# Loads of a streaming kernel in runs of four rows instead of eight

## The chip, the core and the metric

The kernel runs on one core of one Trainium2 chip. The metric is the device time of one execution in microseconds (us); the number that counts is the median of several executions. Engines are called PE (TensorE, the matrix unit), DVE (VectorE), ACT (ScalarE), POOL (GpSimd) and SP (SyncE). Sixteen DMA engines move data between the chip's memory and the core's on-chip memory of 128 partitions.

## The reference

```python
x = -7.109e-05 + 0.9999 * jax.random.normal(..., (128, 128, 1024), jnp.float32)
itok_B_0_7 = jax.random.randint(..., (128,), 0, 8, jnp.int32)
weights = jax.random.normal(kw, (8, 128, 128), dtype=jnp.float32) * (1.0 / 128 ** 0.5)

def reference(x, itok_B_0_7, weights):
    w = weights[itok_B_0_7]
    return x + jnp.einsum('bct,bcd->bdt', x, w)
```

For each of 128 images b, a matrix of 128 channels by 1024 samples, one of eight 128 x 128 weight matrices is picked by an index; the image is multiplied by it and added to the product. Input and output are 64 MiB each, all in 32-bit floats.

## The kernel before

**Tiles and slots.** The 128 images are worked through in 32 tiles of four. A tile is 2 MiB (2.097 MB): two halves (`H = 2`) of two images (`G = 2`). The on-chip buffer `x_all` has 12 slots (`SLOTS`) of one tile each, 16 KB in every partition. A tile is loaded into a slot, multiplied from there into PSUM, copied back from PSUM over its own input in the slot, and stored from there. Tile i + 12 takes the slot of tile i when that is stored.

**Loading** (`load`, L147). Each half is one transfer of 1 MiB, issued by ACT in L72 (`transfer`); it is queue q10 in the profile. In the chip's memory the two images of a half are one unbroken stretch of 256 rows of 4 KB (a row is one channel's 1024 samples). The transfer names the stretch as runs of `ROWS` rows, and the target as 128 partitions with 8 KB each. Eight rows are 32 runs of 32 KB, each written to four partitions in a row. Whatever the run, partition p below 64 gets channels 2p and 2p + 1 of the half's first image, and partition 64 + p those of the second.

**Trading** (`trade`, L162). The multiplication needs the channels of one image spread over all 128 partitions. So ACT exchanges, with five copies in L157 by way of a spare buffer, the second row of the lower 64 partitions for the first row of the upper 64. An image then has its even channels below and its odd ones above; the rows of the weights have been brought into the same order at the start.

**ACT's loop** (L275 to L293). At the start ACT issues the loads of four tiles (`AHEAD = 4`). Then for each tile n it waits until both halves have landed, waits until the slot for tile n + 4 is empty (POOL counts the stores that have landed and raises `s_empty`, L311 to L313), issues the two loads of tile n + 4, and trades tile n. What stands there:

```python
landed(k)
with nc.scalar.If(turn < NT // AHEAD - 1):
    empty = nc.scalar.wait_ge(s_empty, k + 1)
...
    load(k, (turn * AHEAD + (k + AHEAD)) % SLOTS, ...)
trade(k, (turn * AHEAD + k) % SLOTS)
```

**Computing.** DVE adds the picked weight matrix to a unit matrix (`place`, L195 to L200), so that the sum with x comes out of the same product. PE multiplies, 16 matmuls a tile (`multiply`, L202, L208), and DVE copies the product to the slot (`copy`, L217, L223).

**Storing** (`store`, L174). SP waits for DVE and issues the stores; they are in queue q1, as are the weights and indices at the start. Tile 0 goes with a plain transfer (L319), whose pieces are the 4 KB rows of the output. Tiles 1 to 19 go one at a time, 2 MiB in runs of 16 KB (on-chip side), the last twelve in pairs, 4 MiB; the last six tiles (`WHOLE = 6`) are named as runs of 32 KB. In the chip's memory every store writes rows of 4 KB. The end of the program waits for the stores.

Of the kernel before, what the change touches and what calls it, by code (L numbers as in the profile page):

```python
# [45 lines left out]

IDLE = 8

ROWS = 8

R = 2

# [33 lines left out]
def kernel(  # L86
# [60 lines left out]
    def load(k, slot, first):  # L147
        for h in range(H):
# [3 lines left out]
                x_all[:, bass.ds(slot * (H * G * T) + h * G * T, G * T)],  # L152
                x[bass.ds(first + h * G, G)].rearrange("h (b r) t -> (h b) (r t)", r=ROWS),
            ).then_inc(s_in[k], DMA)
# [225 lines left out]
```

## Time and profile before

| what | before |
|---|---|
| median of three executions | 323.84 us (323.23 to 324.43) |
| the profiled execution's own time | 323.75 us |
| its span in the trace | 321.9 us |
| PE busy, share of the span | 247.3 us, 77% |
| ACT busy | 195.7 us, 61% |
| DVE busy | 181.4 us, 56% |
| read and written in the chip's memory | 67.63 MB and 67.11 MB, 419 GB/s over the span |

The profile is of one execution; its own time is 1.85 us more than its span, for what lies around the traced instructions. In the page's second part the span is cut into 40 slices of 8 us, and a digit is the busy share in tenths. In the third part each DMA queue has a row: packets, MB, and the time of its packets as a share of 16 engines' span. A packet is one piece of a transfer on one of the 16 DMA engines; those of a few bytes, 16 to a transfer, carry no data. The same rows can be had for any stretch of the span (a window); a packet is counted in the window in which it begins. "ACTq" and "SPq" are DMA issues of ACT and SP.

### The profile page before, as it was taken

Reading aid. Unit: us, or ns where it says so; the run is one execution under the profiler, and the core shown is the slowest. Engines: PE = TensorE matmul, PEld = TensorE weight load, DVE = VectorE, ACT = ScalarE, POOL = GpSimd, SP = SyncE. Lnnn points to the kernel's source line nnn. Section 1 sums busy time; section 2 is a strip of 40 time slices with the busy share of each in tenths; the row PEclk is TensorE's granted clock in tenths of the full one; section 3 lists DMA queues with packets and bytes.
Section 4 is the critical chain, followed back from the end, with each engine's and each line's share of the span. In section 5 each row is a group of like instructions: output and inputs, shape, how many; then the busy total and the mean of one; then the engine's idle time right before and its main releaser. Section 6 shows DMA issues by size and latency. Waiting matters only on the chain. (4 is left out here: it accounts for less than half of the span.)

```text
span 321.9 us, 2680 instructions
## 1 busy us (share of the span) xinstructions
PE 247.3 (77%) x528; PEld 102.7 (32%) x528; DVE 181.4 (56%) x217; ACT 195.7 (61%) x162; POOL 2.5 (1%) x10
## 2 busy tenths in 40 slices
PE   7279988888888888759949799496784989999000
PEld 3034333333333333324314343242332434443000
DVE  4708765666666666663634847266552676787300
ACT  1577767776777776677275772747727689990000
POOL 0200000000000000000000000000000000000000
PEclk9969999999999999998978979799996999999755
DMA  8999999999999999999999999999999999999995
GB/s 326 391 456 444 405 390 430 438 430 432 417 421 432 425 428 428 432 452 407 425 423 425 423 423 419 421 428 438 446 423 405 432 450 403 428 446 432 419 432 220
DMA packets 7732, 134.76 MB, mean 419 GB/s; under 512 B 1457, under 2 KB 1458, under 8 KB 2098
## 3 DMA queue, kind: packets, MB, share of 16 engines
q1 hardware_dynamic: 4658, 67.64, 49.8%
q10 hardware_dynamic: 3072, 67.11, 49.0%
q14 instruction: 2, 0.02, 0.0%
HBM read 67.63 MB, written 67.11 MB: 419 GB/s over the span
## 5 line engine op out<-in xcount | busy, mean ns | idle before, releaser
L208 PE MATMUL ps<-x_all,w 128*128 x512 | 238.8, 624 | 49.0 <-PEq L204 48.8
L223 DVE COPY x_all<-ps 128x2048 f32 x64 | 146.7, 2292 | 113.7 <-PE ps L208 107.4
L208 PEld LDWEIGHTS ps<-x_all,w 128*128 128x128 f32 x512 | 99.1, 199 | 188.6 <-issue 188.3
L157 ACT COPY aside<-x_all 64x1024 f32 x64 | 66.7, 1042 | 82.4 <-issue 79.1
L157 ACT COPY x_all<-aside 64x1024 f32 x64 | 66.8, 1044 | 1.8
L157 ACT COPY x_all<-x_all x32 | 60.7, 1897 | 3.9
L197 DVE TENSOR_TENSOR w<-w_all,eye 128x128 f32<-128x128 f32 x132 | 31.8, 283 | 0.8 <-issue 0.8
L235 PE MATMUL ps<-x_all 128*128 128x512 f32 x16 | 8.6, 697 | 1.7 <-DVE x_all L232 1.7
L235 PEld LDWEIGHTS ps<-x_all 128*128 128x128 f32 x16 | 3.6, 230 | 5.8 <-issue 4.2
L273 ACT ACT_TABLE_LOAD x1 | 1.3, 1283 | 6.2 <-issue 6.2
L299 DVE COPY w_all<-x_all 32x256 f32<-32x256 f32 x12 | 3.9, 326 | 0.4
L244 DVE STREAM_TRANSPOSE x_all<-x_all 128x512 f32<-128x512 f32 x2 | 2.0, 1076 | 3.1 <-DMA x_all<-in_L_cond_weights_dram 3.1
L299 POOL COPY w_all<-x_all 32x256 f32<-32x256 f32 x4 | 1.7, 425 | 6.6 <-DVE x_all L296 6.4
L296 DVE STREAM_TRANSPOSE x_all<-x_all 128x1024 f32<-128x1024 f32 x1 | 1.2, 1226 | 0.0
L232 DVE MEMSET x_all<- 128x512 f32 x1 | 0.5, 485 | 1.0 <-SPq L225 1.0
L250 DVE TENSOR_SCALAR x_all<-x_all 1x128 int32<-1x128 int32 x1 | 0.2, 215 | 0.3 <-DMA x_all<-in_itok_B_dram 0.3
L260 POOL TENSOR_SCALAR_AFFINE_SELECT eye<-x_all 128x128 f32<-128x128 f32 x1 | 0.3, 292 | 1.4 <-DVE x_all L232 1.4
L254 DVE CUSTOM_DVE_ANT_0 index<-x_all 1x256 uint16<-1x256 uint16 x1 | 0.3, 278 | 0.0
L260 POOL TENSOR_SCALAR_AFFINE_SELECT eye<-eye 128x128 f32<-128x128 f32 x1 | 0.3, 292 | 0.1
L252 DVE TENSOR_SCALAR x_all<-x_all 1x128 int32<-1x128 int32 x1 | 0.2, 215 | 0.0
L273 ACT COPY mark<-eye 1x1 f32<-1x1 f32 x1 | 0.2, 190 | 0.0
L367 POOL MEMSET const-bfloat16-1.0<- 128x1 bf16 x1 | 0.1, 101 | 0.0
(5 smaller groups left out, 0.4 us busy)
## 6 DMA issues: line engine op xcount, KB each, us to landing
x_all<-in_x_dram ACTq DMA_DIRECT2D x64, 1024.0 KB, 11.7
out_dram<-x_all SPq DMA_DIRECT2D x20, 2048.0 KB, 54.1
out_dram<-x_all SPq DMA_DIRECT2D x6, 4096.0 KB, 31.4
x_all<-in_L_cond_weights_dram SPq DMA_DIRECT2D x1, 512.0 KB, 3.8
x_all<-in_itok_B_dram SPq DMA_DIRECT2D x1, 0.5 KB
```

What stands on the lines that cost most here:

```text
L157: nc.scalar.copy(out, in_).then_inc(s_moved, 1)
L197: copy = nc.vector.tensor_tensor(ws[q], w_all[:, bass.ds(subject[q], 1), :], eye, ALU.add)
L208: mm = nc.tensor.matmul(ps[h][:, q % G, t : t + N], ws[q][:, 0, :], x_all[:, bass.ds(at, N)], start=True, stop=True,)
L223: nc.vector.tensor_copy(mine, ps[h].rearrange("d g t -> d (g t)")).then_inc(s_added, 1)
L232: nc.vector.memset(zeros, 0.0).then_inc(s_zeros, 1)
L235: nc.tensor.matmul(ps[P_SLOTS - 1][:, G - 1, :N], zeros[:, :D], zeros, start=True, stop=True)
L244: nc.vector.transpose(w_mid.rearrange("p (e r h w j) -> p r j h e w", e=4, r=R, h=4, w=8)[:, r], w_raw.rearrange("p (j r d) -> p r j d", r ...
L254: nc.vector.tensor_tensor(index[:, :B], near, wrap, ALU.add).then_inc(s_index, 1)
L260: nc.gpsimd.affine_select(eye[:, 0], eye[:, 0] if r else zeros[:, :D], [[-1, D]], ALU.not_equal, 1.0, base=r - r * R * A, channel_multipli ...
L273: nc.scalar.copy(mark, eye[:1, 0, :1])
L296: nc.vector.transpose(w_late, w_mid).then_inc(s_sort, 1)
L299: engine.tensor_copy(w_all[32 * v : 32 * (v + 1), 2 * o : 2 * (o + 1), :], w_late[32 * o : 32 * (o + 1)].rearrange("c (e u r d) -> c u r e ...
```

## The change

```diff
@@ -46,7 +46,7 @@
 
 IDLE = 8
 
-ROWS = 8
+ROWS = 4
 
 R = 2
```

`ROWS` is used in one place, in `load`:

```python
x[bass.ds(first + h * G, G)].rearrange("h (b r) t -> (h b) (r t)", r=ROWS)
```

The source of each of the 64 loads is now 64 runs of 16 KB instead of 32 runs of 32 KB. The target is as before, 128 partitions of 8 KB, so a run is written to two partitions instead of four. Which bytes lie in which partition does not change, and neither does any instruction's place on any engine: number, order and waits are the same.

## The prediction

> **What bounds the kernel now.** I read the page's second part first, for the one resource that has no gap, then its third part for what that resource carries.
>
> ```profile
> DMA  8999999999999999999999999999999999999995
> DMA packets 7732, 134.76 MB, mean 419 GB/s; under 512 B 1457, under 2 KB 1458, under 8 KB 2098
> q1 hardware_dynamic: 4658, 67.64, 49.8%
> q10 hardware_dynamic: 3072, 67.11, 49.0%
> x_all<-in_x_dram ACTq DMA_DIRECT2D x64, 1024.0 KB, 11.7
> out_dram<-x_all SPq DMA_DIRECT2D x20, 2048.0 KB, 54.1
> ```
>
> The 16 DMA engines are busy from the second slice to the last but one. q10 is the loads: 67.11 MB, which is 64 transfers of 1,024 KB. q1 is the stores and, at the start, the weights. Together their packets take 98.8% of 16 engines' span, so all idleness is 1.2% of 321.9 us, 3.9 us. A load lands 11.7 us after its issue, a store 54.1 us after: stores queue up, loads do not. The windows (DMA share last but one, GB/s last) say where the idleness lies.
>
> ```profile
> core 0: us, PE busy (x) PEld busy (x) DVE busy (x) ACT busy (x) POOL busy (x), PEclk, DMA share, GB/s
> 10.00:30.00 20.00, 12.26 (x25) 5.09 (x24) 9.24 (x20) 14.47 (x13) 0.79 (x2) 0.83 1.04 446
> 60.00:120.00 60.00, 52.09 (x119) 21.70 (x118) 38.75 (x45) 43.82 (x37) 0.00 (x0) 1.00 1.00 429
> 120.00:260.00 140.00, 111.70 (x231) 46.21 (x230) 76.56 (x85) 87.30 (x72) 0.00 (x0) 0.91 1.00 425
> 298.00:318.00 20.00, 0.00 (x0) 0.00 (x0) 2.69 (x3) 0.00 (x0) 0.00 (x0) 0.59 0.99 424
> 318.00:321.90 3.90, 0.00 (x0) 0.00 (x0) 0.00 (x0) 0.00 (x0) 0.00 (x0) 0.50 0.06 25
> ```
>
> A share over 1 comes of packets that began in the window and ended behind it. From 10 to 318 us the DMA engines have nothing to spare; TensorE has (52.09 of 60 us), and from 298 us on it does nothing at all while stores drain. So the time is the engines' work divided by 16, plus a start and an end of a few us. A change that adds engine work shows in full; a change that only moves loads and stores against each other shows nothing, as long as one of the two queues always has work.
>
> **The price of one packet.** In these windows one kind of packet runs alone: loads (10 to 30 us), single stores (268 to 288), the last stores, whose runs in the chip's memory are 32 KB long (290 to 318).
>
> ```profile
> DMA packets 400, 8.91 MB, mean 446 GB/s; under 512 B 128, under 2 KB 128, under 8 KB 128
> q10 hardware_dynamic: 400, 8.91, 103.7%
> ...
> DMA packets 555, 8.57 MB, mean 428 GB/s; under 512 B 32, under 2 KB 32, under 8 KB 32
> q1 hardware_dynamic: 555, 8.57, 100.9%
> ...
> DMA packets 398, 11.88 MB, mean 424 GB/s; under 512 B 35, under 2 KB 35, under 8 KB 35
> q1 hardware_dynamic: 398, 11.88, 99.5%
> ```
>
> Without the tiny packets under 512 B, the loads are 400 - 128 = 272 packets for 8.91 MB, 32,768 bytes each: a packet is one run of eight rows, so halving the run should double the packets. One takes 20 x 16 x 1.037 / 272 = 1.220 us on its engine. The single stores are 523 packets of 16,384 bytes, 20 x 16 x 1.009 / 523 = 0.617 us. The last stores are 363 packets of 32,768 bytes, 28 x 16 x 0.995 / 363 = 1.228 us.
>
> **What the change removes and adds.** 64 loads x 32 = 2,048 packets of 32 KB go, 128 on each engine; 4,096 of 16 KB come. No row shows a 16 KB load, so I bound it. Above: the 16 KB store, 0.617 us; two make 1.234, 14 ns over the 1.220 us that they replace, and 128 x 14 ns = 1.8 us. Below: two halves cost what the whole did, 0 us. Less than nothing would need a 16 KB packet under 0.610 us, and no row has one. Between the two, by how many pieces a packet is written in: the 32 KB store goes to eight pieces of 4 KB and takes 8 ns longer than the 32 KB load, which goes to four of 8 KB; that is an estimated 2 ns a piece. The new load writes two pieces where the 16 KB store writes four, so 0.617 - 0.004 = 0.613 us, 2 x 0.613 - 1.220 = 6 ns for each old packet, and 128 x 6 ns = 0.8 us. I take 0.9 us, a little towards the row that is nearest, and keep 0 to 1.8.
>
> The Trainium skill, page "DMA: Bandwidth & Descriptors", section "Why small descriptors are slow (HBM only)", speaks against the change too, but by less: it states a fixed overhead of about 3 cycles for each packet on trn2. At the 850 MHz that the same page's section "Where 436 GB/s comes from" gives for the fabric, 128 more packets on an engine would cost an estimated 0.45 us and the forecast would be 0.45 us lower. That overhead alone gives 3.5 ns where the stores' rows leave room for 14, so the rows decide.
>
> **Do the two queues hinder each other when mixed?** This matters because loads and stores will alternate more finely.
>
> ```profile
> DMA packets 1406, 25.72 MB, mean 429 GB/s; under 512 B 304, under 2 KB 304, under 8 KB 304
> q10 hardware_dynamic: 692, 15.34, 59.6%
> q1 hardware_dynamic: 714, 10.39, 40.8%
> ```
>
> In 60 to 120 us, 15.34 MB are 468 loads of 32 KB, 60 x 16 x 0.596 / 468 = 1.223 us each, and 10.39 MB are 634 stores, 0.618 us each: the prices of the runs alone. I cost the alternation at nothing.
>
> **What moves: the shares.** When both queues have work, how is it divided? From 31 to 36 us the loads still have a backlog and the first store, the only one cut into 4 KB packets, has just begun.
>
> ```profile
> DMA packets 119, 1.88 MB, mean 375 GB/s; under 512 B 19, under 2 KB 19, under 8 KB 67
> q10 hardware_dynamic: 70, 1.67, 80.2%
> q1 hardware_dynamic: 48, 0.20, 9.8%
> ```
>
> 1.67 MB is 51 loads of 32 KB, beside 48 stores of 4 KB: a packet each in turn, whatever its size. So a load of 32 KB now has two thirds of the engines against 16 KB stores; with 16 KB it will have half. ScalarE issues a tile's two loads when an earlier tile lands and a slot is free:
>
> ```profile
> 43.01 1.27 ACTq L72 DMA_DIRECT2D x_all<-in_x_dram  x2
> ...
> 51.24 1.31 ACTq L72 DMA_DIRECT2D x_all<-in_x_dram  x2
> ...
> 59.51 1.16 ACTq L72 DMA_DIRECT2D x_all<-in_x_dram  x2
> ...
> 67.70 1.15 ACTq L72 DMA_DIRECT2D x_all<-in_x_dram  x2
> ```
>
> A tile every 8.2 us. Its four packets per engine take 4 x (1.220 + 0.617) = 7.3 us in turns with stores, so the load queue empties before the next tile. After the change eight turns take 8 x (0.613 + 0.617) = 9.8 us: loads will queue, ScalarE will in the end wait for landings, and stores will get through sooner. If issuing a load with twice the runs costs ScalarE more, that is covered: even doubled (1.15 us more per tile) its turn of 8.2 us stays under 9.8. Only the very first issue has nothing before it; I allow 0.6 us for that at the top of the range.
>
> None of this costs time unless both queues run dry before the end. The danger is the end, so I work out how far loads will be ahead of stores.
>
> ```profile
> q10 hardware_dynamic: 538, 11.96, 90.1%
> ...
> q1 hardware_dynamic: 142, 0.58, 14.5%
> ...
> x_all<-in_x_dram ACTq DMA_DIRECT2D x20, 1024.0 KB, 12.2
> ...
> q1 hardware_dynamic: 1059, 22.07, 93.7%
> q10 hardware_dynamic: 14, 0.00, 0.0%
> ...
> 283.77 2.11 ACT L157 COPY aside<-x_all 64x1024 f32 x2 [0.51 <-ACTq L160]
> ...
> 301.24 0.56 SPq L72 DMA_DIRECT2D out_dram<-x_all  x1
> ```
>
> The first row is 0 to 31 us: 11.96 MB are loaded when the first store begins. The second is 31 to 41 us: 142 packets of the first store, 4 KB each, take 10 x 16 x 0.145 / 142 = 0.163 us. The third is 0 to 56 us: 20 loads, ten tiles, are issued. The next two are 266.7 us to the end: now all loads are in by 266.7 us and 22.07 MB, 10.5 tiles of 2.097 MB, are still to be stored. The last two are the last tile's trade and the last store's issue, 17.5 us apart.
>
> After the change the first store's 512 packets of 4 KB are 32 turns on each engine. They take 32 x (0.613 + 0.163) = 24.8 us, in which 512 loads of 16 KB bring 8.39 MB. At 56 us 20.3 MB are loaded (the ten tiles issued are 20.97 MB, so the queue does not run dry) and 2.1 MB stored: 18.2 MB, 8.7 tiles, ahead. From there both sides move 16 KB a turn and the lead stays 8.7 tiles; with 12 slots some 3.3 tiles of loads remain queued, so the load queue stays full. Stores alone take 8 packets of 32 KB per engine and pair of tiles, 8 x 1.228 = 9.8 us, 4.9 us a tile, so the last load lands 8.7 x 4.9 = 43 us before the end, at some 279 us, and the last store can be issued at about 279 + 17.5 + 0.6 = 297 us. It needs 9.8 us, to 307; the stores ahead of it keep the engines busy until about 322 - 9.8 = 312. Nothing shows.
>
> **The sum.** The profiled execution took 323.75 us, 1.85 more than its span. Plus 0.9 it is 324.65 us. The median of the three runs is 323.84, 0.09 above it; for the measured time I give 324.7 us.
>
> **The rivals.** (1) The engines run dry at the end. Last trade to end of last store is 17.5 + 0.6 + 9.8 = 28 us, 5.7 tiles of stores. If the lead after the change falls below 5.7 tiles, each missing tile costs 4.9 us. Loads build most of their lead against the small packets of the first store; if they gained nothing there, the lead would stay at what was loaded by 31 us, 11.96 / 2.097 = 5.7 tiles, just at that point, and whenever the load queue was then empty for a moment it would shrink. One tile less is 4.9 us lost, 329.6 us. For it: the share of the loads does fall, and ScalarE's wait for landings is new. Against it: 3 tiles of margin, and the 51 to 48 packets. Chance 0.1. The Trainium skill, same page, section "Queues, rings and completion order", would rule it out: an engine drains a whole packet, typically 9 to 17 descriptors, from one queue before it turns, so a load's share would hang less on the length of its run. The row of 51 to 48 shows turns of one run each; I go by it.
> (2) The change does not reach the engines, because a transfer of 1 MB is cut as before: 323.8 us. Against it, 32,768 bytes is exactly the run in the code. Chance 0.07.
> (3) Packets of 16 KB are cheaper as loads than any row shows, or finer alternation helps: at 0.600 us a packet, 128 x 20 ns = 2.6 us less, 321.2 us. Against it, mixed and unmixed packets cost the same now. Chance 0.05.
>
> **How the numbers follow.** The forecast, 324.7 us, has 0.78, with a range of its own from 323.8 to 325.6, or 326.2 with the first issue. A difference of 0.5%, 1.6 us, is about what a measurement of this kernel can tell from no change; the three runs lie 1.2 us apart. So slower takes rival (1) and the upper end of the forecast, 0.1 + 0.13 = 0.23; faster is rival (3), 0.05; the rest is 0.72. The range, 323.2 to 326.8 us, holds the forecast, its bounds with the runs' spread, and rival (2), and leaves out most of rivals (1) and (3).
>
> **What would show it.** Right: 4,096 packets of 16 KB in q10 with a price of 0.610 to 0.617 us; the two queues' shares together up by some 0.9 us of span; loads landing far later than 11.7 us and stores sooner than 54.1; the last load near 279 us instead of 266.7; a DMA row without a new gap. Wrong: a 0 or a low digit in the DMA row ahead of the last slice (rival 1), q10 with 32 KB packets as before (rival 2), or a 16 KB load under 0.610 us (rival 3).

## The result and the profile after

The changed kernel takes 335.75 us (median of six runs, 334.82 to 336.24), the kernel before 323.31 us on the same chip (six runs, 322.84 to 324.43). The ratio is 1.0378, with a 95% interval of 1.0365 to 1.0391: 12.4 us slower. The profiled execution took 336.02 us, its span is 334.2 us.

The page of the changed kernel comes first, with the same rows that the prediction showed of the kernel before.

```profile
DMA  7999999999999999999999999999999999997047
DMA packets 9780, 134.76 MB, mean 403 GB/s; under 512 B 1457, under 2 KB 1458, under 8 KB 2098
q1 hardware_dynamic: 4658, 67.64, 47.8%
q10 hardware_dynamic: 5120, 67.11, 47.2%
x_all<-in_x_dram ACTq DMA_DIRECT2D x64, 1024.0 KB, 25.7
out_dram<-x_all SPq DMA_DIRECT2D x20, 2048.0 KB, 35.6
```

q10 has 2,048 packets more, so the runs did reach the engines as packets of 16 KB. Both queues together take 95.0% of 334.2 us, 317.5 us, against 98.8% of 321.9, 318.0 us, before: within the rounding of these shares (0.05% of the span each) the engines have no more work than they had. What is new is the 0 near the end of the DMA row, where the kernel before had nines. The windows show it in microseconds.

```profile
core 0: us, PE busy (x) PEld busy (x) DVE busy (x) ACT busy (x) POOL busy (x), PEclk, DMA share, GB/s
10.00:300.00 290.00, 233.33 (x491) 96.08 (x490) 164.78 (x193) 188.18 (x155) 0.34 (x1) 0.94 1.01 428
300.00:308.00 8.00, 3.67 (x9) 1.33 (x7) 5.38 (x6) 4.93 (x4) 0.00 (x0) 0.90 0.93 395
308.00:322.00 14.00, 8.92 (x16) 3.63 (x16) 5.38 (x6) 1.14 (x2) 0.00 (x0) 0.82 0.01 2
322.00:334.20 12.20, 0.00 (x0) 0.00 (x0) 0.00 (x0) 0.00 (x0) 0.00 (x0) 0.56 0.80 344
```

Up to 300 us the engines run as before. From 308 to 322 us they move nothing: 14 us, a little more than the kernel lost. In that stretch PE does its 16 matmuls of the last tile. These are the last instructions of ACT and SP around it; the three points stand for rows left out:

```profile
302.90 2.11 ACT L157 COPY aside<-x_all 64x1024 f32 x2 [9.66 <-ACTq L160]
...
321.70 0.56 SPq L72 DMA_DIRECT2D out_dram<-x_all  x1
```

ACT waits 9.66 us for the last tile to land (L160 is `landed`) and trades it at 302.90; the last store goes out at 321.70. All other stores were done well before it went out. This is what the first rival of the prediction described: the engines run dry at the end. What remains is why the last load landed at some 301 us, and not at 279 as forecast. The window of 70 to 270 us of the changed kernel, in which both queues have work, answers it.

```profile
DMA packets 6174, 85.69 MB, mean 428 GB/s; under 512 B 944, under 2 KB 944, under 8 KB 944
q1 hardware_dynamic: 3087, 45.34, 53.4%
q10 hardware_dynamic: 3087, 40.36, 47.3%
```

The number of packets is the same in both queues, to the last one, but only if the packets of a few bytes are counted. (Of the data alone it is 40.36 MB / 16,384 = 2,463 packets against 2,767.) So a queue gets one packet in its turn, and the few bytes with which each transfer ends on each engine are a packet like any other; they are called ending packets below. A tile's data is 2,097,152 / 16 = 131,072 bytes on an engine. With four-row loads that is eight packets, and two transfers end: ten turns, 13.1 KB a turn (a KB here is 1,000 bytes). A tile stored alone is eight packets and one end: nine turns, 14.6 KB. The rows have 40.36 MB / 3,087 = 13.1 KB and 45.34 / 3,087 = 14.7 KB. With eight-row loads a tile has 4 + 2 = 6 turns, by the same count 21.8 KB a turn. Before, loads outran stores (15.34 MB against 10.39 in 60 to 120 us); now stores outrun loads by some 12%, and the lead of the loads melts.

The lead, loaded less stored tiles, can be followed in three windows of the changed kernel: 0 to 56 us, 280 to 300.8 us, and 300.8 us to the end.

```profile
q10 hardware_dynamic: 1455, 19.12, 80.9%
q1 hardware_dynamic: 735, 3.62, 16.8%
...
q1 hardware_dynamic: 240, 6.26, 70.6%
q10 hardware_dynamic: 225, 2.90, 32.7%
...
q1 hardware_dynamic: 242, 6.88, 48.4%
q10 hardware_dynamic: 1, 0.00, 0.0%
```

At 56 us it is 19.12 - (3.62 - 0.52 of weights) = 16.0 MB, 7.6 tiles, where 8.7 were forecast. From 70 to 270 us stores gain 45.34 - 40.36 = 4.98 MB, 2.4 tiles. From about 280 us on the last six tiles are being stored in runs of 32 KB, twice the size of a load's, and in 21 us stores gain another 6.26 - 2.90 = 3.36 MB, 1.6 tiles. Another 0.4 tiles go in the two short stretches between (56 to 70 and 270 to 280 us). When the last load has landed, 6.88 MB are left, 3.3 tiles. The prediction put the point of decision at 5.7 tiles and 4.9 us on each that is missing: (5.7 - 3.3) x 4.9 = 11.8 us. The loss is 12.4 us.

### The profile page after: what moved, and what is told of

Same layout as the page of the kernel before. It is cut to its first block, busy times and chain, and to the rows that moved or that the text cites. A ratio compares the mean times of both kernels' runs of the same rounds, so it can differ in the third digit from the quotient of the medians.

```text
span 334.2 us, 2680 instructions
## 1 busy us (share of the span) xinstructions
PE 254.2 (76%) x528; PEld 104.7 (31%) x528; DVE 181.2 (54%) x217; ACT 195.7 (59%) x162; POOL 2.5 (1%) x10
## 5 line engine op out<-in xcount | busy, mean ns | idle before, releaser
L208 PE MATMUL ps<-x_all,w 128*128 x512 | 245.0, 635 | 62.6 <-PEq L204 62.6
L208 PEld LDWEIGHTS ps<-x_all,w 128*128 128x128 f32 x512 | 100.9, 202 | 206.6 <-issue 206.5
L235 PE MATMUL ps<-x_all 128*128 128x512 f32 x16 | 9.3, 742 | 1.7 <-DVE x_all L232 1.7
## 6 DMA issues: line engine op xcount, KB each, us to landing
x_all<-in_x_dram ACTq DMA_DIRECT2D x64, 1024.0 KB, 25.7
out_dram<-x_all SPq DMA_DIRECT2D x20, 2048.0 KB, 35.6
```

The source lines that it names most:

```text
L208: mm = nc.tensor.matmul(ps[h][:, q % G, t : t + N], ws[q][:, 0, :], x_all[:, bass.ds(at, N)], start=True, stop=True,)
L235: nc.tensor.matmul(ps[P_SLOTS - 1][:, G - 1, :N], zeros[:, :D], zeros, start=True, stop=True)
```

## The experiments

Theory T: engines serve the two queues a packet in turn, the ending packets counted; four-row loads therefore lose the lead that eight-row loads build, the last tile lands late, and the engines stand dry while it is traded, multiplied and copied. Rival P: loads in short runs are slow by themselves. Rival S: shares are even, and only the 32 KB stores at the end take the loads' turns.

Each ratio below is to the kernel before as measured together with that run: 323.53 us for the first four runs, 323.81 us for the last four. What a run loses or gains is taken from there.

**The last stores in shorter runs.** On the changed kernel:

```diff
-WHOLE = 6
+WHOLE = 0
```

> Four-row loads as in the changed kernel, and the last six tiles are stored in runs of 16 KB instead of 32 KB. Theory T (each queue gets one packet in turn, the few-byte completion packets included; the loads of the changed kernel therefore fall behind the stores, the last tile lands late, and the engines run dry while it is computed): from 280 us on, loads keep their 203 KB per ns-ten-thousandth share, that is 2.03 MB in 10 us instead of 1.4, so the 2.90 MB that land after 280 us need 14 us instead of 20; the last load at about 294 us, the time about 330 us (329 to 332). Rival P (loads in 16 KB runs are slow by themselves, whatever the stores do): no change, 335.8 us. Rival S (only the 32 KB stores at the end take the loads' share; before that queues share evenly): nearly all of the loss goes, 325 us.

(The garbled "203 KB per ns-ten-thousandth share" stands for 203 GB/s, which is 2.03 MB in 10 us.) Measured: 330.65 us (327.98 to 331.74), ratio to the kernel before 1.0201 (1.014 to 1.0261). The window 280 to 296.5 us of this run:

```profile
q1 hardware_dynamic: 268, 4.13, 58.8%
q10 hardware_dynamic: 227, 2.93, 41.7%
```

The 2.93 MB are in after some 16 us instead of 20.8 (T had expected 14), and the loss falls from 12.4 to 7.1 us, by 5.3. The time lies in T's range of 329 to 332 us. P, which expected no gain, does not fit, and neither does S, by which nearly all would have come back.

**Stores in runs of 8 KB.** On the changed kernel, in `store`:

```diff
-                "d (o t) -> d o t", o=1 if i >= NT - WHOLE else n
+                "d (o t) -> d o t", o=n * 2
```

> Four-row loads, and every store from tile 1 on is cut into runs of 8 KB, half of before. Theory T: a tile of loads is 8 + 2 turns, of stores 16 + 1, so loads get 13.1 KB a turn against 7.7 and never fall behind; no dry stretch; 323.3 plus 0.8 us for the loads' packets and some 2 us for the stores' additional packets: 326 us (325 to 328). Rival P: not under 335.8, and about 338 with the stores' shorter runs. Rival S: 326 us as well.

Measured: 323.22 us (323.07 to 323.73), ratio 0.9990 (0.9978 to 1.0002). The whole loss is gone, although the loads are those of the changed kernel and only the stores were cut. Its page:

```profile
DMA  7999999999999999999999999999999999999995
q1 hardware_dynamic: 9010, 67.64, 50.2%
q10 hardware_dynamic: 5120, 67.11, 49.1%
x_all<-in_x_dram ACTq DMA_DIRECT2D x64, 1024.0 KB, 11.4
out_dram<-x_all SPq DMA_DIRECT2D x20, 2048.0 KB, 54.1
```

Loads land after 11.4 us and stores after 54.1, much as they did before the change. So P falls; S expected the same as T here. The 2 to 3 us that were expected for the additional packets did not come, and the time lies below T's range of 325 to 328 us.

**Four more turns behind each store.** Run lengths stay as in the changed kernel. SP issues a transfer of 48 pieces of 4 bytes from `weights` to an unused buffer (declared with its semaphore in lines not shown); nothing of the computation changes.

```diff
                 store(i, n).then_inc(s_slot[i % SLOTS], DMA)
+                transfer(
+                    nc, nc.sync, tiny[:, i : i + 1], weights[0, :48, :1]
+                ).then_inc(s_tiny, DMA)
```

> Four-row loads and stores as in the changed kernel; behind each store from tile 1 on SP issues one transfer of 192 bytes, which puts three packets of 4 bytes and a completion packet on each engine's store queue. No run length changes. Theory T: a single store has 13 turns instead of 9, a pair 21 instead of 17, so loads (10 turns a tile) get 13.1 KB a turn against 10.1 (12.5 in pairs) and no longer fall behind; no dry stretch, or one of a few us; 325 us (324 to 328). Rivals P and S: packets of a few bytes do not count, 335.8 us or a little more.

Measured: 323.27 us (323.11 to 323.41), ratio 0.9989 (0.9978 to 1.0000). Its window of 70 to 270 us, and then 269 us to the end:

```profile
q10 hardware_dynamic: 3423, 44.81, 52.5%
q1 hardware_dynamic: 3999, 40.70, 48.2%
...
q1 hardware_dynamic: 1270, 20.89, 92.9%
```

Now loads move more than stores, though no run has another length than in the changed kernel, and by 269 us all loads are in, with 20.89 MB, ten tiles, left to store. (The counts are not equal here; the loads of this run land 11.9 us after their issue, as before the change, so the load queue is at times empty.) Packets that carry next to nothing take away the whole loss of 12.4 us, which of the three only T allows. The time, 323.27 us, is below T's range of 324 to 328 us.

**Eight-row loads with four more turns.** This is the reverse, on the kernel before: ACT issues the same small transfer behind the two loads of each tile.

```diff
             ).then_inc(s_in[k], DMA)
+        transfer(
+            nc, nc.scalar, tiny[:, bass.ds(at, 1)], weights[0, :48, :1]
+        ).then_inc(s_tiny, DMA)
```

> Eight-row loads and stores as in the kernel before; behind the two loads of each tile ACT issues one transfer of 192 bytes, three packets of 4 bytes and a completion packet on each engine's load queue. Theory T: a tile of loads has 4 + 2 + 4 = 10 turns, as many as with four-row loads, and so the same 13.1 KB a turn against the stores' 14.6; the loads fall behind, the last load lands near 300 us, and the time is that of the changed kernel less its 0.8 us of packets: 335 us (332 to 337). Rivals P and S: runs of 32 KB are what they were, 323.3 to 324.5 us.

Measured: 336.38 us (334.09 to 336.91), ratio 1.0378 (1.0327 to 1.043), the same ratio as that of the change. Its page's DMA row, the window of 70 to 270 us, and 303 us to the end:

```profile
DMA  8999999999999999999999999999999999979147
...
q1 hardware_dynamic: 3062, 45.19, 53.2%
q10 hardware_dynamic: 3075, 40.31, 47.5%
...
q1 hardware_dynamic: 259, 7.44, 55.2%
```

The loads are those of before, 32 KB a packet; the turns are those of the change, and so are the bytes (45.19 to 40.31 MB, in 3,062 to 3,075 packets) and the time, with a 1 in the DMA row where the engines stand dry at the end. The length of the runs matters here only through the number of turns.

**Runs of two rows.**

```diff
-ROWS = 4
+ROWS = 2
```

> Loads in runs of two rows, 8 KB, half again; stores as in the changed kernel. Theory T: a tile of loads is 16 + 2 turns and the loads' share falls further, but stores can only go out for tiles that have been loaded and computed, so the loss has a floor that the changed kernel has nearly reached: when the last load lands, the last two pairs at the most are left to store. 67.1 + 0.5 + 58.7 MB have then passed at 0.4285 MB per us, with 2.5 us for the additional packets some 300 us, and the rest takes the 35 us that it takes in the changed kernel: 335 us (333 to 338). Rival P (short runs are slow by themselves): at least another 12 us, twice that for twice the packets: 348 to 360 us.

Measured: 336.93 us (335.62 to 338.21), ratio 1.0418 (1.0372 to 1.0463): a loss of 13.1 us, which its interval does not tell from the 12.4 of four rows. Its page:

```profile
DMA  7999999999999999999999999999999999999047
q10 hardware_dynamic: 9216, 67.11, 47.8%
x_all<-in_x_dram ACTq DMA_DIRECT2D x64, 1024.0 KB, 31.4
out_dram<-x_all SPq DMA_DIRECT2D x20, 2048.0 KB, 12.9
```

A store now lands 12.9 us after its issue: there is hardly a backlog of stores left to lose, and the gap cannot grow much. The time lies in T's range; P, by which each halving costs another 12 us or more, is out.

**The last pair split.** On the changed kernel, tiles 30 and 31 are stored one by one, each when DVE is done with it (the wait for the stores at the end is changed to match):

```diff
+            if i + n == NT:
+                nc.sync.wait_ge(s_added, (NT - 1) * H)
+                store(i, 1).then_inc(s_slot[i % SLOTS], DMA)
             nc.sync.wait_ge(s_added, (i + n) * H)
...
-    last = store(NT - PAIR, PAIR)
+    last = store(NT - 1, 1)
```

> Four-row loads; the last pair of tiles is stored as two tiles, each when it is ready, so that only 2.1 MB wait for the last tile instead of 4.2. Theory T: at the end the engines are dry until the last tile is computed, so tile 30 is stored in the dry time, and the last store takes 4.9 us instead of 9.8: 335.75 less 4.9 is 330.9 us (329.5 to 332). Rival P: the engines' work is what it was, 335.8 us.

Measured: 331.26 us (330.19 to 332.12), ratio 1.0227 (1.0195 to 1.026): a loss of 7.5 us, 5.0 less than the changed kernel's. With the 16 KB runs at the end as well:

> Four-row loads, the last pair split as in the run before, and the last six tiles stored in runs of 16 KB instead of 32. Theory T: the two repairs act on different terms, the landing of the last load and the chain behind it, so they add up: 330.65 (16 KB runs alone) less 4.9 is 325.8 us (324 to 327.5). Rival P: 330 us or more.

Measured: 325.10 us (322.90 to 326.06), ratio 1.0028 (0.9999 to 1.0057). The two repairs gained 5.3 and 5.0 us one by one and 11.2 together; the runs of this one spread over 3 us, so the sum fits. The control is the split on the kernel before:

> The kernel before, eight-row loads, with the last pair split. A control for the split. Theory T: with eight-row loads the engines never run dry, so a shorter last store brings nothing: 323.4 us (322.9 to 324). If the split helps here too, its gain with four-row loads is not that of the dry time.

Measured: 323.67 us (322.95 to 324.11), ratio 0.9996 (0.9986 to 1.0007). A shorter chain behind the last load gains where the engines are dry, and nothing where they are not. The DMA rows are from the pages of the split alone, of the split with 16 KB runs, and of the control:

```profile
DMA  7999999999999999999999999999999999999905
...
DMA  7999999999999999999999999999999999999976
...
DMA  8999999999999999999999999999999999999995
```

No version beats the kernel before: the stores of 8 KB and the additional turns behind the stores come back to it, and its engines have hardly any time left to win.

## Why the prediction was wrong

**What bounds the kernel: right.** The engines' packets fill the span but for a start and an end, and a gap at the end shows in full. Loads now queue and stores get through sooner, as forecast: they land after 25.7 and 35.6 us, where it was 11.7 and 54.1.

**The price of the packets: too high.** 0.9 us were forecast, 317.5 against 318.0 us of engine work were measured, and the run with four more turns, which has the same loads, is not slower than the kernel before. Over the whole span a 32 KB load took 321.9 x 16 x 0.490 / 2,048 = 1.232 us before, and a 16 KB load takes 334.2 x 16 x 0.472 / 4,096 = 0.616 us now: two of them 1.232, which adds nothing: the lower bound, 0 us, that the prediction gave for this term. The new price lies in the forecast's 0.610 to 0.617 us. The old one, 1.220 us, was too low: it came from one short window, and the windows differ by about as much as the 6 to 14 ns that the estimate turned on. The prediction's own mixed window, 60 to 120 us, had 1.223 us. From before, 120 to 260 us:

```profile
q10 hardware_dynamic: 1376, 29.89, 50.2%
```

29.89 MB are 912 loads, 140 x 16 x 0.502 / 912 = 1.233 us each. (The 32 KB runs of the last stores, which the prediction puts in the chip's memory, are on the on-chip side; in the chip's memory every store writes rows of 4 KB. Its estimate of 2 ns a piece goes by those rows.) The Trainium skill, page "DMA: Bandwidth & Descriptors", section "Why small descriptors are slow (HBM only)", would have asked for an estimated 0.45 us more. No run here shows even that.

**The shares: the step that failed.** "From there both sides move 16 KB a turn and the lead stays 8.7 tiles". It rested on 51 load packets beside 48 of the store, counted without the packets of a few bytes, in a window that had begun before the first store reached the engines. From before, 33.2 to 42 us, when both queues had work:

```profile
DMA packets 290, 3.75 MB, mean 426 GB/s; under 512 B 48, under 2 KB 48, under 8 KB 192
q10 hardware_dynamic: 144, 3.15, 84.3%
q1 hardware_dynamic: 144, 0.59, 16.6%
```

144 to 144, the 48 small ones of the loads included. That row was there to be read before the change was tried, and ten turns against nine follow from it. The lead did not stay 8.7 tiles: it was 3.3 when the last load was in, at 300.8 us instead of 279. Of the 5.4 tiles that are missing, 1.0 were so at 56 us, 2.8 went from there to 280 us, where stores moved some 12% more than loads, and 1.6 after that. The rule of the Trainium skill, same page, section "Queues, rings and completion order", that an engine drains a whole packet of typically 9 to 17 descriptors before it turns, does not agree with these rows: one run, or one ending packet, is a turn.

**The lead at 56 us: 7.6 tiles instead of 8.7.** This is for the most part the same step. The changed kernel's window of 31 to 56 us, for which the forecast had 512 loads, 8.39 MB, and 2.1 MB stored:

```profile
q10 hardware_dynamic: 568, 7.41, 71.2%
q1 hardware_dynamic: 589, 3.10, 29.8%
```

7.41 MB are 452 loads; the other 116 turns of the queue are ending packets, which the forecast left out. And the queue did run dry: ScalarE had issued ten tiles by 52.5 us, but from 53.2 to 56 us the load queue has 32 packets beside 82 of the store queue.

**The stores of 32 KB.** With a lead of 8.7 tiles these last six would have begun after the last load. With the lead that was left they began before it, and took another 1.6 tiles. The run with 16 KB stores at the end puts 5.3 us on this.

**The rival's mechanism: right in place, and near in point and price,** 5.7 tiles and 4.9 us a tile. That it comes within 0.6 us here is in part luck. The chain that it is made of was longer, 321.70 - 302.90 = 18.8 us from the last trade to the last issue where 17.5 were taken. With eight-row loads and more turns 7.90 MB, 3.8 tiles, were left when the last load was in, at 302.6 us; the rule gives 9.3 us there, and 12.9 were lost. The rival had a chance of 0.1, because three tiles looked like margin; a loss that goes on for 200 us was not weighed against it.

## What to carry to other kernels

In these traces, where both queues have work, each gets one packet in its turn (3,087 to 3,087 in 200 us): the bytes of a queue per turn, with each transfer's ending packet counted as a turn, set how the bandwidth is divided (13.1 KB against 14.7, and 40.36 MB against 45.34). Shortening one side's runs cost nothing that could be measured as engine work here, and 12.4 us as share; if loads then fall behind stores, the last tile comes late and its whole chain stands bare at the end. A lead that melts by some ten per cent has to be followed to the last load, not judged where it is built.

## What was not expected of the hardware

The packets of a few bytes that end a transfer take a turn of the queue like a packet of 16 KB (3,087 to 3,087 packets in 200 us) or of 32 KB (144 to 144 in 8.8 us). 24 transfers of 192 bytes in the store queue took away the whole loss of 12.4 us, and 32 of them in the load queue of the kernel before brought 12.9 us. Twice the packets cost the engines nothing that could be measured: 317.5 us of work against 318.0, and 323.22 us with about twice the data packets in both queues against 323.53 for the kernel before, on the same chip.
